# A macaron layer of two feed-forward passes and an S4D mixer: no side work behind the last two tiles of an ordinary block's second wide layer, and steps one fourteenth larger

## The chip, the core and the metric

The kernel runs on one core of a Trainium2 chip. The time is that of the device for one execution, in microseconds (us). A core has five engines that matter here, each with its own queue of instructions, taken in order: TensorE (PE in the profile; its weight loads are PEld), VectorE (DVE), ScalarE (ACT), GpSimd (POOL), and SyncE (SP), which only issues DMAs here. They run side by side and wait for one another through semaphores.

## The reference

The input x is (4, 1024, 256): four sequences of 1,024 tokens with 256 channels. Three residual steps follow one another:

```
x = x + 0.5 * ffn(layernorm(x))
x = x + mix(layernorm(x))
x = x + 0.5 * ffn(layernorm(x))

ffn(x):   h = silu(x @ w1.T * s1) * (x @ w2.T * s2)    # 256 -> 1024
          h = gelu(h @ h1.T * s_h1)                    # 1024 -> 1024
          h = gelu(h @ h2.T * s_h2)                    # 1024 -> 1024
          return h @ w3.T * s3                         # 1024 -> 256
mix(x):   K[d, l] = 2 Re sum_n C'[d, n] exp(dtA[d, n] * l)
          y = irfft(rfft(x, 2L) * rfft(K, 2L))[:L]     # along the tokens, L = 1024
          return gelu(y) @ W.T + b
```

Both passes have the same weights. All matrices of the ffn are ternary (-1, 0, 1). Everything is float32, and the gelu is the exact one.

## The kernel before

**Blocks.** Each ffn pass is cut into eight blocks of 512 tokens: f0 to f7 in the first pass, g0 to g7 in the second. They are worked one after another: f0 to f7, g0, g1 as ordinary blocks (`ffn`), then (g2, g3), (g4, g5), (g6, g7) as pairs (`ffn_pair`), which save matmuls by a product of Strassen's kind. Activations are held with features on the 128 partitions and the 512 tokens along the free axis. A wide layer (1,024 features) is thus eight tiles of 128 x 512, m = 0 to 7.

**A wide tile.** Each activation is kept as two tiles for TensorE's fp32r format: a high part, which is a cast of the value, and a low part, which is the value less the high part. Since the weights are ternary, a matmul with each part gives the product to about the accuracy of float32. `linear` (L363) issues for a tile of layer 2 or 3 16 matmuls (eight blocks of input features, two parts each) into one bank of PSUM, L366. ScalarE then takes the gelu (L399), ScalarE casts it to the high part (L401), VectorE subtracts for the low part (`low_part`, L309). In layer 1 there are two banks, `pa` and `pb`, of eight matmuls in all; silu is L384, the product with `pb` L385, the cast L389. Tiles are named by layer and block: p2_f0_3, g2_f0_3, h2_f0_3 are the bank, the gelu and the two parts of tile 3 of layer 2 in f0. The profile leaves the numbers out: p_f, g_f, h_f, and ha_f for layer 1.

**The end of a block.** `last_squares` (L604 to L632) multiplies the eight tiles of layer 3 by w3: two banks `po`, 16 matmuls each, L617. ScalarE scales them (L628), VectorE transposes (L629), POOL adds the residual (L630), and stores follow. The next block's layer 1 comes right after `po` on TensorE; its operand xt is cut into parts by `parted` (casts L356, low parts L309), once the last tile of the block before is done.

**Side work.** All else is done beside the wide tiles of ordinary blocks. After each tile of layers 2 and 3 two things are called:

- `ahead()` moves the preparation of the next block on by one step: load of x, mean and variance on VectorE (L155), the root for them on ScalarE (`rstd`, L289), scaling (L155), transposes into squares of 32 (`sq`) and a way through DRAM (L339).
- `tick()` (L1237) hands out a portion of the rest. The rest is a generator, `aside`: `kernel_steps`, the table of powers for the S4D kernel (during f0 to f2); its spectrum; and for each of the four sequences `mix`, as soon as its two f blocks are done. `fillers` (checks that the weights are what the kernel takes them for) fill up where `aside` has nothing.

The part of `kernel_steps` that runs in f0's layer 3 is `powers`: for a group of channels an angle `a` and a factor `e` on VectorE, an exp on ScalarE (L820), the reduction of the angle in four VectorE operations with `k` as helper, a sine and a cosine on ScalarE (L740, L741), the products with `e` and with `c_dt`, and from them the tiles `qd`. The names are e_0_0, a_0_0, k_0_0 for the fine powers and e_b_0, a_b_0, k_b_0, then e_b_32, a_b_32, k_b_32, qd_32, qd_48 for the coarse ones. Gelu, sine, exp and root each have a table of their own in ScalarE; where one follows another, an ACT_TABLE_LOAD stands between them.

How much a tick hands out is a matter of counting: every VectorE operation of side work adds OP_WORK (130) and its columns to `work_done` (L144 to L153), and a tick runs the generator

```
allowed = min(allowed, work_done) + (STEP_WORK_2 if f7 is done else STEP_WORK)
while work_done < allowed:   next(aside) ...
```

The order of the instructions on each engine is then set by the scheduler of the language, which takes the program in this order and may put an instruction ahead of others on its engine when it reckons that it is ready earlier; pools of 19 `half` tiles and 15 `ring` tiles bound how far ahead.

At the end of the program a flag tells whether a weight was not ternary; then everything is run again in a plainer way. With these inputs it is not.

Of the kernel before, what the change touches and what calls it, by code (L numbers as in the profile page):

```python
# [23 lines left out]
KH = HID // P  # L24
# [10 lines left out]

STEP_WORK, STEP_WORK_2, OP_WORK, MIN_WORK = 3600, 3400, 130, 300
PAUSE = "pause"
N_CHECKS = 44  # L40

# [67 lines left out]
def macaron_layers(  # L109
# [54 lines left out]
    def bank(name):  # L164
        return psum.tile([P, 512], F32, tag="ps", name=name)

    def half(name, *shape, dtype=F32):

        return work.tile([P, *(shape or (512,))], dtype, tag="half", name=name, bufs=19)

    def ring(name, *shape, dtype=F32):

        return work.tile([P, *shape], dtype, tag="ring", name=name, bufs=15)
# [133 lines left out]
    def low_part(t, src):  # L307

        return nc.vector.tensor_tensor(t[:, 1, :], src, t[:, 0, :].bitcast(F32), ALU.subtract)  # L309
# [52 lines left out]
    def linear(ps, w, m, acts):  # L362
        n = len(acts)  # L363
        for k in range(n):
            for part in range(parts):
                nc.tensor.matmul(  # L366
                    ps,
                    w[:, k, m * P : (m + 1) * P],
                    acts[k][:, part, :],
                    start=(k == 0 and part == 0),  # L370
                    stop=(k == n - 1 and part == parts - 1),
                )

    def ffn(xt, src, dst, blk, name, tick, ahead, final):


        ha = []
        for m in range(KH):
            pa, pb = bank(f"pa_{name}_{m}"), bank(f"pb_{name}_{m}")
            linear(pa, w1_sb, m, xt)  # L380
            linear(pb, w2_sb, m, xt)
            g = half(f"g_{name}_{m}")
            t = ring(f"ha_{name}_{m}", parts, TB, dtype=wide)
            nc.scalar.activation(g, pa, AF.Silu, scale=sc_sb[:, 0, m : m + 1])  # L384
            nc.vector.scalar_tensor_tensor(  # L385
                g if split else t[:, 0, :], pb, sc_sb[:, 1, m : m + 1], g, ALU.mult, ALU.mult
            )
            if split:
                nc.scalar.copy(t[:, 0, :], g)  # L389
                low_part(t, g)  # L390
            ha.append(t)
        for layer, w in ((2, h1_sb), (3, h2_sb)):
            hb = []
            for m in range(KH):
                ps = bank(f"p{layer}_{name}_{m}")
                linear(ps, w, m, ha)
                t = ring(f"h{layer}_{name}_{m}", parts, TB, dtype=wide)
                g = half(f"g{layer}_{name}_{m}") if split else t[:, 0, :]
                nc.scalar.activation(g, ps, AF.Gelu, scale=sc_sb[:, layer, m : m + 1])  # L399
                if split:  # L400
                    nc.scalar.copy(t[:, 0, :], g)  # L401
                    low_part(t, g)
                hb.append(t)
                ahead()
                if layer == 2 or m < KH - 1:
                    tick()
            ha = hb
        ahead(last=True)
        if name == "f0":
            nc.scalar.mul(w3s_half, w3s_half, 0.5)  # L410
        if final:
            last_tokens(ha, src, dst, blk, name)
        else:
            last_squares(ha, src, dst, blk, name)()
# [188 lines left out]
    def last_squares(acts, src, dst, blk, name, first=0):  # L603


        rest = []
        for k in range(DC):
            xr = half(f"xr_{name}_{k}", TB // SQ, SQ)
            for c in range(P // SQ):
                nc.sync.dma_start(xr[c * SQ : (c + 1) * SQ], in_squares(src, blk, k, c))  # L610
            rest.append(xr)
        banks = [bank(f"po_{name}_{k}") for k in range(DC)]
        order = [(first + k) % KH for k in range(KH)]
        for o, ps in enumerate(banks):
            for k in order:
                for part in range(parts):
                    nc.tensor.matmul(  # L617
                        ps,
                        w3_sb[:, k, o * P : (o + 1) * P],
                        acts[k][:, part, :],  # L620
                        start=(k == order[0] and part == 0),
                        stop=(k == order[-1] and part == parts - 1),
                    )

        def end():
            for k, ps in enumerate(banks):
                o, y = half(f"o_{name}_{k}"), half(f"y_{name}_{k}", TB // SQ, SQ)
                nc.scalar.activation(o, ps, AF.Identity, scale=w3s_half[:, k : k + 1])  # L628
                nc.vector.transpose(y, o.rearrange("p (n s) -> p n s", s=SQ))  # L629
                nc.gpsimd.tensor_tensor(y, rest[k], y, ALU.add)  # L630
                for c in range(P // SQ):
                    stores.dma_start(in_squares(dst, blk, k, c), y[c * SQ : (c + 1) * SQ])  # L632

        return end

    def last_tokens(acts, src, dst, blk, name):

        rest = {}
        for i in (0, 2):
            rest[i] = half(f"xr_{name}_{i}", 2, D)  # L640
            nc.sync.dma_start(rest[i], tokens(src, blk, i, 2))

        def result(ps, i, n):

            for e in range(n):
                for k in range(KH):
                    for part in range(parts):
                        nc.tensor.matmul(  # L648
                            ps[:, e * D : (e + 1) * D],
                            acts[k][:, part, (i + e) * P : (i + e + 1) * P],  # L650
                            w3_sb[:, k, :],
                            start=(k == 0 and part == 0),
                            stop=(k == KH - 1 and part == parts - 1),
                        )

        def finish(ps, y, xr, i, n, add_on):
            nc.vector.scalar_tensor_tensor(
                y,
                ps.rearrange("p (e d) -> p e d", e=n),
                0.5,  # L660
                w3s_sb[:, None, :].to_broadcast([P, n, D]),
                ALU.mult,
                ALU.mult,
            )
            add_on.tensor_tensor(y, xr, y, ALU.add)
            nc.sync.dma_start(tokens(dst, blk, i, n), y)

        y = half(f"y_{name}_0", 2, D)
        ps = bank(f"po_{name}_0")
        result(ps, 0, 2)  # L670
        finish(ps, y, rest[0], 0, 2, nc.gpsimd)
        y = half(f"y_{name}_2", 2, D)
        for e in range(2):
            ps = bank(f"po_{name}_{2 + e}")
            result(ps, 2 + e, 1)
            finish(ps[:, 0:D], y[:, e : e + 1, :], rest[2][:, e : e + 1, :], 2 + e, 1, nc.vector)
# [568 lines left out]
    def tick():  # L1245


        nonlocal ticks, allowed, work_done
        ticks += 1
        allowed = min(allowed, work_done) + (  # L1250
            STEP_WORK_2 if ("f", n_blocks - 1) in done else STEP_WORK
        )
        while work_done < allowed:
            at = work_done
            if next(aside, PAUSE) is PAUSE:
                for _ in range(2):
                    if len(done) > 8 and allowed - work_done > OP_WORK + TB:
                        next(fillers, None)
                break
            if work_done == at:  # L1260
                work_done += MIN_WORK
# [10 lines left out]
    for n, unit in enumerate(units):  # L1272
# [6 lines left out]
        def ahead(last=False):  # L1279
            if last:  # L1280
                done.extend(("last layer", *b[::-1]) for b in upcoming)
            for step in steps:
                next(step, None)
# [15 lines left out]
        with tc.issue_after(last_split.ins) if n == 0 else nullcontext():  # L1299
            if pair:  # L1300
                blks = [b for _, b in unit]
                ffn_pair(operands, src, dst, blks, names, tick, ahead, final)
            else:
                ffn(operands[0], src, dst, blk, names[0], tick, ahead, final)
# [81 lines left out]
```

## Time and profile before

| | |
|---|---|
| median of the runs | 1368.81 us (1368.12 to 1369.08, 3 runs) |
| the profiled execution | 1368.22 us, its span 1366.4 us |
| mean granted TensorE clock | 0.999 of full speed |
| L366 (wide layers of ordinary blocks), each matmul 128x128 by 128x512 | 391 ns mean |
| L617 `po_f` matmuls | 256, 60.7 us busy |
| ACT_TABLE_LOAD before L399, L289, L384, L820, L740 | 35, 19, 10, 8, 8 of them, 1283 ns each |

The span is the time between the first and the last instruction that the profile shows; the execution's own time has some two microseconds around it. Busy times of TensorE are modelled: matmuls are pipelined, one lasts 391 ns from its start to its modelled end, but the next starts 227 ns after it. Lines of groups give the line of the source, the engine, the operation, output<-input, sizes and number, and after the bar busy time, mean duration, and the idle time before them with what ended it. Lines of waits give engine, tile and line, what was waited for, then microseconds in total, times, and the longest.

### The profile page before, as it was taken

The page shows a single profiled execution, that of the slowest core. Times are in us where ns is not written, and L with a number is a line of the kernel's source. Part 1 is how long each engine was busy: PE and PEld are TensorE (multiplying, and loading weights), DVE is VectorE, ACT ScalarE, POOL GpSimd, SP SyncE. Part 2 cuts the span into 40 slices and gives each one's busy share as a digit, 9 for nine tenths or more (in the row PEclk, how much of TensorE's full clock was granted, in tenths as well). Part 3 has the DMA queues.
Part 4 walks back from the last instruction along what each step waited for, and adds up shares of the span by engine and source line. Part 5 has one row for each costly group of instructions (what it writes and reads, how often), then busy time and mean ns, then how long its engine had stood idle before and what let it go on. Part 6 is the DMA issues. An engine that isn't in the chain of part 4 may idle for free.

```text
span 1366.4 us, 18201 instructions
## 1 busy us (share of the span) xinstructions
PE 1351.8 (99%) x6300; PEld 1125.2 (82%) x6300; DVE 1008.8 (74%) x1886; ACT 776.4 (57%) x1236; POOL 297.1 (22%) x454
## 2 busy tenths in 40 slices
PE   9999999999999999999999999999999999999997
PEld 7888878888888888887888887888888888888886
DVE  6997885749865887668855799658885778568654
ACT  5985966454444543534545745436776476656663
POOL 4440220421205213420214012052300430040002
PEclk9999999999999999999999999999999999999999
DMA  9440121414125236454054342352655145521441
GB/s 354 114 141 3 31 62 39 146 33 124 39 93 204 59 108 188 125 183 120 20 169 115 115 154 47 115 166 83 208 165 168 31 139 181 170 66 62 160 148 34
DMA packets 121670, 160.00 MB, mean 117 GB/s; under 512 B 73872, under 2 KB 84112, under 8 KB 116192
## 3 DMA queue, kind: packets, MB, share of 16 engines
q1 hardware_dynamic: 99296, 99.41, 23.8%
q0 software_dynamic: 22000, 59.07, 13.9%
q8 instruction: 51, 0.84, 0.3%
q14 instruction: 51, 0.42, 0.1%
q10 hardware_dynamic: 272, 0.26, 0.1%
HBM read 120.95 MB, written 37.75 MB: 116 GB/s over the span
## 4 chain that ended last, share of the span: by engine, by line
PE 50%; DVE 4%; issue 1%; DMA 0%; ACT 0%; SPq 0%; DVEq 0%; POOLq 0%; POOL 0%; ACTq 0%
PE p_g L366 7%; PE p3a_g L510 6%; PE p2a_g L510 6%; PE p2x_g L510 5%; PE p3x_g L510 5%; PE p_f L366 4%; PE pa_g L366 4%; PE pb_g L366 4%; PE po_g L617 3%; PE pi L1134 1%; PE pw L1159 1%; DVE y L155 1%; PE po_f L617 1%; PE po_g L648 1%; PE pa_f L366 1%; PE pb_f L366 1%
## 5 line engine op out<-in xcount | busy, mean ns | idle before, releaser
L366 PE MATMUL p_f<-ha_f,h_sb 128*128 128x512 f32 x1024 | 238.7, 392 | 0.1
L366 PE MATMUL p_f<-h_f,h_sb 128*128 128x512 f32 x1024 | 237.1, 391 | 0.0
L366 PEld LDWEIGHTS p_f<-h_f,h_sb 128*128 128x128 f32 x1024 | 192.1, 188 | 39.7
L366 PEld LDWEIGHTS p_f<-ha_f,h_sb 128*128 128x128 f32 x1024 | 191.4, 188 | 40.4 <-DVE ha_f L309 0.8
L399 ACT ACTIVATE g_f<-p_f,sc_sb 128x512 f32<-128x512 f32 x128 | 87.4, 689 | 210.2 <-PE p_f L366 178.6
L309 DVE TENSOR_TENSOR h_f<-g_f,h_f 128x512 fp32r<-128x512 f32 x128 | 88.1, 691 | 113.4 <-ACT h_f L401 113.2
L630 POOL TENSOR_TENSOR y_g<-xr_g,y_g 128x512 f32<-128x512 f32 x14 | 19.9, 1431 | 323.8 <-DVE y_g L629 310.1
L401 ACT CAST h_f<-g_f 128x512 fp32r<-128x512 f32 x128 | 78.4, 619 | 3.1
L524 ACT ACTIVATE h_g<-h_g,sc_sb 128x512 f32<-128x512 f32 x72 | 52.0, 724 | 43.9 <-DVE h_g L480 43.6
L339 POOL DMA_DIRECT2D moved<-sq_f x56 | 30.6, 554 | 197.8 <-DVE sq_f L155 197.8
L366 PE MATMUL pa_f<-xt_f,w_sb 128*128 128x512 f32 x256 | 70.5, 391 | 1.8 <-DVE xt_f L356 1.2
L339 POOL DMA_DIRECT2D moved<-sq_g x64 | 34.9, 552 | 167.5 <-DVE sq_g L155 166.3
L366 PE MATMUL pb_f<-xt_f,w_sb 128*128 128x512 f32 x256 | 70.0, 389 | 0.0
L366 PE MATMUL pa_g<-xt_g,w_sb 128*128 128x512 f32 x256 | 68.9, 389 | 0.0
L366 PE MATMUL pb_g<-xt_g,w_sb 128*128 128x512 f32 x256 | 68.9, 389 | 0.0
L617 PE MATMUL po_f<-h_f,w_sb 128*128 128x512 f32 x256 | 60.7, 391 | 1.6 <-ACT h_f L401 0.9
L385 DVE SCALAR_TENSOR_TENSOR g_f<-pb_f,sc_sb,g_f 128x512 f32<-128x512 f32 x64 | 46.6, 746 | 19.7 <-ACT g_f L384 10.0
L366 PE MATMUL p_g<-ha_g,h_sb 128*128 128x512 f32 x256 | 59.4, 391 | 0.1
L366 PE MATMUL p_g<-h_g,h_sb 128*128 128x512 f32 x256 | 59.3, 391 | 0.0
L366 PEld LDWEIGHTS pa_f<-xt_f,w_sb 128*128 128x128 f32 x256 | 48.0, 188 | 12.8 <-DVE xt_f L356 1.6
L617 PEld LDWEIGHTS po_f<-h_f,w_sb 128*128 128x128 f32 x256 | 47.6, 188 | 13.0 <-DVE h_f L309 2.0
L399 ACT ACTIVATE g_g<-p_g,sc_sb 128x512 f32<-128x512 f32 x32 | 22.1, 690 | 60.8 <-PE p_g L366 50.3
(302 smaller groups left out, 2887.9 us busy)
## 6 DMA issues: line engine op xcount, KB each, us to landing
w<-q SPq DMA_DIRECT2D x42, 1024.0 KB, 5.0
q<-s POOLq DMA_DIRECT2D x40, 256.0 KB, 4.4
h_sb<-in_h_dram POOLq DMA_DIRECT2D x8, 1024.0 KB, 14.4
given<-in_h_dram SPq DMA_DIRECT2D x32, 256.0 KB, 3.4
kr<-k_hat SPq DMA_DIRECT2D x20, 256.0 KB, 2.8
ki<-k_hat SPq DMA_DIRECT2D x20, 256.0 KB, 3.1
q<-h_sb POOLq DMA_DIRECT2D x16, 256.0 KB, 4.8
xr_f<-in_x_dram SPq DMA_DIRECT2D x64, 64.0 KB, 2.5
```

What stands on the lines that cost most here:

```text
L155: return op(dst, *args, **kwargs)
L309: return nc.vector.tensor_tensor(t[:, 1, :], src, t[:, 0, :].bitcast(F32), ALU.subtract)
L339: stores.dma_start(moved[k].rearrange("(c r) a q -> a r c q", r=SQ)[a], sq[a * SQ : (a + 1) * SQ].rearrange("r c j s -> r c (j s)"),)
L366: nc.tensor.matmul(ps, w[:, k, m * P : (m + 1) * P], acts[k][:, part, :], start=(k == 0 and part == 0), stop=(k == n - 1 and part == parts ...
L385: nc.vector.scalar_tensor_tensor(g if split else t[:, 0, :], pb, sc_sb[:, 1, m : m + 1], g, ALU.mult, ALU.mult)
L399: nc.scalar.activation(g, ps, AF.Gelu, scale=sc_sb[:, layer, m : m + 1])
L401: nc.scalar.copy(t[:, 0, :], g)
L510: nc.tensor.matmul(ps, weights[:, c, m * P : (m + 1) * P], ops[c][:, part, :], start=(first and c == 0 and part == 0), stop=(c == QK - 1 a ...
L524: nc.scalar.activation(o, src, AF.Gelu, scale=sc_sb[:, layer, m : m + 1])
L617: nc.tensor.matmul(ps, w3_sb[:, k, o * P : (o + 1) * P], acts[k][:, part, :], start=(k == order[0] and part == 0), stop=(k == order[-1] an ...
L630: nc.gpsimd.tensor_tensor(y, rest[k], y, ALU.add)
L648: nc.tensor.matmul(ps[:, e * D : (e + 1) * D], acts[k][:, part, (i + e) * P : (i + e + 1) * P], w3_sb[:, k, :], start=(k == 0 and part == ...
```

## The change

In an ordinary block, a tick followed each of the 16 wide tiles of layers 2 and 3 but the last: 15 ticks. Now none follows the last two: 14 ticks. The portion of a tick grows by about a fourteenth, from 3,600 to 3,850 units, and after f7 from 3,400 to 3,640. `ahead()` is called after every tile as before. The pair blocks have ticks of their own, with the larger portion too.

```diff
-STEP_WORK, STEP_WORK_2, OP_WORK, MIN_WORK = 3600, 3400, 130, 300
+STEP_WORK, STEP_WORK_2, OP_WORK, MIN_WORK = 3850, 3640, 130, 300
...
                     low_part(t, g)
                 hb.append(t)
                 ahead()
-                if layer == 2 or m < KH - 1:
+                if layer == 2 or m < KH - 2:
                     tick()
             ha = hb
         ahead(last=True)
```

## The prediction

> **What bounds the kernel now.** I read the page first, then the waits of TensorE, then the queues of the engines around the ends of the ordinary blocks. From the page:
>
> ```profile
> span 1366.4 us, 18201 instructions
> ...
> PE 1351.8 (99%) x6300; PEld 1125.2 (82%) x6300; DVE 1008.8 (74%) x1886; ACT 776.4 (57%) x1236; POOL 297.1 (22%) x454
> ...
> PE   9999999999999999999999999999999999999997
> ...
> ACT  5985966454444543534545745436776476656663
> ...
> L399 ACT ACTIVATE g_f<-p_f,sc_sb 128x512 f32<-128x512 f32 x128 | 87.4, 689 | 210.2 <-PE p_f L366 178.6
> L309 DVE TENSOR_TENSOR h_f<-g_f,h_f 128x512 fp32r<-128x512 f32 x128 | 88.1, 691 | 113.4 <-ACT h_f L401 113.2
> ```
>
> TensorE is full in every slice, and neither the number nor the size of its matmuls changes. So only the time in which it stands still can change. ScalarE and VectorE have room on the average, but the third ACT digit (68 to 102 us, the end of block f0 in it) is an 8 after a 9: there ScalarE is nearly full. The waits of TensorE that belong to ends of blocks:
>
> ```profile
> PE pa_f L366 <- DVE xt_f L356: 1.2, 1, 1.2
> PE po_f L617 <- ACT h_f L401: 0.9, 1, 0.9
> PE po_f L617 <- DVE h_f L309: 0.7, 1, 0.7
> PE po_g L617 <- DVE h_g L309: 0.6, 1, 0.6
> PE po_g L617 <- ACT h_g L401: 0.3, 1, 0.3
> ```
>
> They are small. Matmuls start 0.2267 us apart (64 of them fill 14.52 us in the chain), so the 32 of `po` need 7.25 us. Laid against the starts in the timeline, which also shows what the pipelined ends hide, the ends of blocks stand still for 0.35 (f0), 2.15 (f1), 0.06 (f4), 1.42 (f6) and 1.47 us (g0), and the starts of layer 2 in f1 and g1 for 0.48 and 0.36. That is 5.45 us at block ends: all that the change can win by its own idea, 6.3 with the two starts. One such end, f1, in TensorE's timeline (start, length):
>
> ```profile
> 171.46 6.51 PE L617 MATMUL po_f<-h_f,w_sb 128*128 128x512 f32 x28
> 178.86 0.73 PE L617 MATMUL po_f<-h_f,w_sb 128*128 128x512 f32 x2 [0.89 <-ACT h_f L401]
> 180.31 0.72 PE L617 MATMUL po_f<-h_f,w_sb 128*128 128x512 f32 x2 [0.72 <-DVE h_f L309]
> ```
>
> 28 matmuls run, the last four wait for the last tile of layer 3: its cast, then its low part.
>
> **What a last tile needs.** Gelu 0.69, cast 0.62 and low part 0.69 us end 2.26 us after the tile's last matmul if nothing else stands in the queues. 14 matmuls of the next stage can run before it is needed (3.17 us). So side work put between these three costs nothing up to 0.9 us, and more when earlier matmuls can be put ahead.
>
> **The change, part by part.** A tick lets side work run until 3,850 units instead of 3,600 are counted (3,640 instead of 3,400 after f7). Over a block it is 14 x 3,850 = 53,900 against 15 x 3,600 = 54,000: as much work, 250 units more per tile. A 512-column VectorE operation counts 642 and starts 0.60 us after its predecessor, so a tile gets about 0.25 us more, and the tile m=6 of layer 3 gives up about 3.4. No matmul and no VectorE, POOL or SP operation is added or removed. What is added are ScalarE's table loads, 92 to 96 in the built program: f4 +3, f6 and g0 +2 each, g1 +1, less two each in f2 and g2; f0 keeps 22, in another order. A load takes 1.28 us (below), so 5 us more on an engine with 590 us idle; it costs only where a wide tile waits behind it. On TensorE some 130 of 5,892 instructions change places, among them the 16-matmul groups of the mix (3.45 us each, f5's last into f6's layer 2, g1's from layer 3 into layer 2); they take the same time there. On SP and POOL the same DMAs are issued, some in another order: the last quarter of x_f3 ahead of stores of squares, the kr, ki, given and xr loads up to a tile earlier or past one another. These land 2.5 to 3.4 us after their issue and are read a tile (3.63 us) or more later; I cost them at nothing, and at one such landing, 3.4 us, if a late one ever stood ahead of a low part.
>
> The scheduler decides the order on each engine, so I walked the queues of the built program with durations of this trace: gelu 0.69 (0.59 behind another), cast 0.62, table load 1.28, sine pair 1.25, exp 0.63, root 0.30; VectorE 0.69 (0.60), `qd` 0.43, x_f3's scaling 0.33.
>
> *Blocks f1, f6, g0 (the gain).* In f1 the sine group of tile 5 is issued one tile earlier, so the low parts of tiles 6 and 7 come at 177.85 and 178.45 instead of 178.9 and 180.25; they are needed at 176.9 and later, which leaves 0.6 of the 2.15: **-1.5**. In f6 the two stand at 641.3 and 641.9, needed at 642.5 and 643.6, and the cast of `xt_f7` is ahead of them now: **-1.4**. In g0, 826.0 and 826.6, needed from 825.1: some 0.55 left of 1.47: **-0.9** (-1.5 to +0.5, since ScalarE gets two loads more there). f4: **-0.06**. No other block end stood still, and none does in the walk.
>
> *Block f0 (the loss).* Here it is ScalarE's order that counts. Its timeline at the end of f0 before:
>
> ```profile
> 82.78 1.28 ACT L289 ACT_TABLE_LOAD   x1
> 84.08 0.30 ACT L289 ACTIVATE rstd_f<-mv_f,eps 128x4 f32<-128x4 f32 x1
> 84.28 0.61 ACT L401 CAST h_f<-g_f 128x512 fp32r<-128x512 f32 x1
> 84.91 1.28 ACT L740 ACT_TABLE_LOAD   x1
> 86.20 0.63 ACT L740 ACTIVATE a_b<-a_b 128x512 f32<-128x512 f32 x1
> 86.74 0.71 ACT L741 ACTIVATE k_b<-k_b,cst_sb 128x512 f32<-128x512 f32 x1
> ```
>
> The cast at 84.28 is h3_f0_7's; the sine pair of a_b_32, k_b_32 and the root of f3 come behind it, at no cost. In the built program both stand ahead of g3_f0_6, because the larger step of tile 5 reaches them. Between the first gelu of layer 3 and that last cast there are 11 table loads instead of 8 (+3.9 us), three sine pairs instead of two (+1.25) and two roots instead of one (+0.3): +5.45. And the stretch starts later. The exp e_0_0 with its two loads moves ahead of g2_f0_7, so h2_f0_7 is ready near 62.95 instead of 58.58; TensorE's order allows for that with 46 matmuls ahead of its first use (63.3) instead of 27. So TensorE does not wait, but p3_f0_0 closes only then, and ScalarE's layer 3 starts at 64.4 instead of 60.3 (+4.1). Its idle bits of before (0.74) are filled. The last cast ends at 84.9 + 4.1 + 5.45 - 0.74 = 93.7, that of tile 6 at 93.2. On VectorE the sine pair's products, the rest of x_f3 and four `qd` (4.4 us, from 90.4) stand ahead of the low parts of tiles 6 and 7: ready at 95.5 and 96.1. TensorE finishes p3_f0_7 at 81.9 and the 24 matmuls of tiles 0 to 5 near 88.5, since tile 5's own low part comes at 87.5; stands still to 93.3, again to 95.5, and leaves `po` near 97.1 instead of 89.48: **+7.7**. Both ends: +5.5 if VectorE gets round to the low parts as soon as the casts are there (tail 93.7 + 0.69 + 0.6), +9.3 if h2_f0_7 is 1.5 us later than walked. The walk's own bookkeeping stands nearer the middle, which I take. Then f0's side work no longer reaches into f1, whose start loses its 0.48: **-0.45**.
>
> *The clock.* No gap of TensorE exceeds 1.4 us before, so the trace shows what a long one does only at its end:
>
> ```profile
> core 0: us, PE busy (x) PEld busy (x) DVE busy (x) ACT busy (x) POOL busy (x), PEclk, DMA share, GB/s
> ...
> 1355.00:1360.00 5.00, 3.86 (x33) 3.65 (x31) 2.39 (x5) 0.00 (x0) 3.86 (x5) 1.00 0.33 87
> 1360.00:1366.00 6.00, 0.00 (x0) 0.00 (x0) 0.00 (x0) 0.00 (x0) 0.00 (x0) 0.76 0.27 73
> ```
>
> The last matmul ends at 1358.9; a mean of 0.76 over six us is full clock to about 1363.1 and half after: 4.3 us of idleness. The gap foreseen at f0 is 4.8. The Trainium skill ("TensorE: Matmul & The Clock Gate", What's actually happening) puts the drop to half at an idle window of about 3.4 us and the return after a busy one as long. By the page the gap trips for certain, and a 3.4 us window at half speed loses 1.7. By the row it trips just barely or not: 0. At most two windows, 3.4. I take **+1.0**.
>
> *The loads.* The Trainium skill ("ScalarE: Activation LUTs", What ACT_TABLE_LOAD costs) gives 1.28 us and a drain of 1.38 for every switch, which speaks against this change: three switches more in f0 would be 8.0 us instead of 3.9, the sum +8.5. In the timeline above the next operation follows 0.02 us behind the load (84.08, 86.20), so there is no drain here, and I take 1.28.
>
> **The sum.** +7.7 - 0.45 - 1.5 - 0.06 - 1.4 - 0.9 = +3.4, with the clock +4.4. On the profiled execution, 1368.22 (span 1366.4 and 1.8 around it), 1372.6; that execution lies 0.6 under the median of the runs, 1368.81, which the prediction goes by: **1373.2 us**. The pair blocks keep TensorE's order, and by then no side work is left for a tick.
>
> **Rivals.** *A: the change does what it says everywhere*, f0 too: the tiles before last find empty queues and 4.6 to 5.4 us of waits go: about 1364, faster. For it: f1, f6 and g0 in the waits. Against it: the ScalarE order in f0. It decides if f0's `po` ends by 93 instead of 97.1; below that the gains outweigh it.
>
> *B: f0 loses less*, +5.5, because VectorE is not behind, and the clock holds: +1.2, about 1370, not to be told from no change (0.2%, 2.7 us, is about what a measurement of this kernel can tell). For it: VectorE has 26% idle over the span. Against it: it is busy throughout 52.9 to 82 in f0.
>
> *C: larger steps are late elsewhere too.* Before the last tile of layer 2 the walk leaves 0.2 us in f5 and g0 and 0.5 for tile 6 in f7: a load more ahead of one costs about 1 us each, and the clock its two windows: +3.4 + 2 + 2.4 to 3.4, about 1377. Against it: these waits are filled in TensorE's order by the next tile's first 14 to 18 matmuls.
>
> **How the numbers follow.** Likeliest (1371.5 to 1375.5) 0.52; B 0.22; C 0.16; A 0.08; the rest, 0.02, further up. Range: half of B and nearly all of C stay in it, 1368.4 to 1377.6. Faster: A, 0.08. Within 0.2% (1366.1 to 1371.5): B, 0.22. Slower: 0.70.
>
> **What would show it.** In the profile after: a wait of `po_f` for h_f of about 4.8 us and a second of about 2.2, both in f0 (88 to 97 us); `po_g` and `pa_f <- xt_f L356` waits gone or under 0.6; f1's `po` below 0.7; a granted clock under 1.00 in a window of 90 to 102 us if the clock term is real. Wrong would be: no wait over 3 us near 90 (then A or B), a full clock through 90 to 102 (then about 1372), or new waits at starts of layer 3 (C).

## The result and the profile after

| | before | after |
|---|---|---|
| median of the runs | 1368.9 us (1368.12 to 1370.22, 8 runs) | 1373.51 us (1373.05 to 1374.58, 8 runs) |
| ratio to before | | 1.0033, 95% interval 1.0024 to 1.0041 |
| the profiled execution, its span | 1368.22, 1366.4 us | 1374.58, 1372.8 us |
| granted clock, mean of the span | 0.999 | 0.994 |

The changed kernel is 4.6 us slower by the medians; its profiled execution is the slowest of the eight, so the two spans lie 6.4 us apart. Its page, the lines that answer to those of before:

```profile
span 1372.8 us, 18195 instructions
...
PE 1354.4 (99%) x6300; PEld 1126.8 (82%) x6300; DVE 1007.2 (73%) x1886; ACT 780.4 (57%) x1240; POOL 297.5 (22%) x454
...
PE   8989999999999999999999999999999999999997
...
ACT  5785875454363543544544746345776566656663
PEclk9989999999999999999999999999999999999999
```

TensorE's third slice (69 to 103 us) is an 8, and so is the clock's. ScalarE has four instructions more, the table loads. The waits of TensorE:

```profile
PE po_f L617 <- ACT h_f L401: 4.6, 1, 4.6
...
PE po_f L617 <- DVE h_f L309: 2.3, 3, 1.0
...
PE po_g L617 <- DVE h_g L309: 0.3, 1, 0.3
```

One wait of 4.6 us is new. The small ones have shrunk: `po_g` is down to 0.3, `pa_f <- xt_f L356` of 1.2 is gone. TensorE's timeline puts the new wait at the end of f0:

```profile
82.11 4.54 PE L617 MATMUL po_f<-h_f,w_sb 128*128 128x512 f32 x18
87.24 1.66 PE L617 MATMUL po_f<-h_f,w_sb 128*128 128x512 f32 x6 [0.58 <-DVE h_f L309]
93.46 1.22 PE L617 MATMUL po_f<-h_f,w_sb 128*128 128x512 f32 x2 [4.57 <-ACT h_f L401]
95.63 2.93 PE L617 MATMUL po_f<-h_f,w_sb 128*128 128x512 f32 x6 [0.95 <-DVE h_f L309]
98.36 1.91 PE L366 MATMUL pa_f<-xt_f,w_sb 128*128 128x512 f32 x4
```

Layer 1 of f1 starts at 98.36; before it started at 89.48. The last two lines show a second thing: six matmuls of `po` take 2.93 us, and the next four matmuls begin 0.427 us apart, not 0.227. The granted clock says why. In the windows below the columns are the length, the busy time of TensorE, its weight loads, VectorE, ScalarE and POOL (with their instructions in brackets), then the clock, and last what the DMAs did:

```profile
84.00:88.00 4.00, 3.40 (x14) 2.19 (x13) 4.00 (x9) 3.95 (x7) 0.00 (x0) 1.00 0.00 0
88.00:92.00 4.00, 0.89 (x4) 0.40 (x3) 3.96 (x10) 3.96 (x5) 0.00 (x0) 0.88 0.72 114
92.00:96.00 4.00, 1.59 (x3) 0.87 (x4) 3.93 (x9) 1.92 (x4) 0.00 (x0) 0.50 0.11 17
96.00:100.00 4.00, 4.00 (x10) 3.10 (x10) 3.43 (x7) 2.08 (x3) 1.16 (x1) 0.50 0.00 0
100.00:104.00 4.00, 4.00 (x16) 3.21 (x15) 1.11 (x3) 1.97 (x3) 3.69 (x6) 0.84 0.32 66
```

The clock is halved from 91.0 to 101.3 us. From 84 to 92 VectorE and ScalarE are full, and TensorE waits for them. ScalarE's timeline up to the cast that ends the long wait:

```profile
86.17 1.28 ACT L289 ACT_TABLE_LOAD   x1
87.47 0.30 ACT L289 ACTIVATE rstd_f<-mv_f,eps 128x4 f32<-128x4 f32 x1
87.78 1.28 ACT L740 ACT_TABLE_LOAD   x1
89.08 0.63 ACT L740 ACTIVATE a_b<-a_b 128x512 f32<-128x512 f32 x1
89.61 0.71 ACT L741 ACTIVATE k_b<-k_b,cst_sb 128x512 f32<-128x512 f32 x1
90.34 1.28 ACT L399 ACT_TABLE_LOAD   x1
91.63 1.26 ACT L399 ACTIVATE g_f<-p_f,sc_sb 128x512 f32<-128x512 f32 x2
92.79 1.13 ACT L401 CAST h_f<-g_f 128x512 fp32r<-128x512 f32 x2
```

Root and sine pair with three table loads stand ahead of the gelus of tiles 6 and 7, whose matmuls had ended at 78.7 and 82.3.

### The profile page after: what moved, and what is told of

Read it like the earlier page. It is cut to its first block, busy times and chain, and to the rows that moved or that the text cites. A ratio compares the mean times of both kernels' runs of the same rounds, so it can differ in the third digit from the quotient of the medians.

```text
span 1372.8 us, 18195 instructions
## 1 busy us (share of the span) xinstructions
PE 1354.4 (99%) x6300; PEld 1126.8 (82%) x6300; DVE 1007.2 (73%) x1886; ACT 780.4 (57%) x1240; POOL 297.5 (22%) x454
## 4 chain that ended last, share of the span: by engine, by line
PE 86%; DVE 5%; issue 1%; ACT 1%; POOL 0%; DVEq 0%; POOLq 0%; ACTq 0%
PE p_f L366 27%; PE p2a_g L510 6%; PE p3a_g L510 6%; PE p_g L366 6%; PE p3x_g L510 5%; PE p2x_g L510 5%; PE pa_g L366 4%; PE pb_g L366 4%; PE pa_f L366 4%; PE pb_f L366 4%; PE po_f L617 4%; PE po_g L617 3%; PE pi L1134 2%; PE pf_m L956 2%; PE pw L1159 2%; PE pk L883 1%
```

## The experiments

All were timed beside runs of the kernel before on the same chip (median 1369.15 to 1369.49), so ratios compare best. The theory: f0 alone loses, because larger steps put the exp and the sine pair a tile earlier; the ends of f1, f6 and g0 gain; a halved clock adds to the loss. The rivals are that the loss is spread over the blocks, that leaving out the tick is to blame, that one engine alone sets f0's end, and that the clock costs nothing.

| kernel | median, us | ratio, 95% interval |
|---|---|---|
| the change (measured again) | 1373.34 | 1.0030 (1.0019 to 1.0042) |
| everywhere but in f0 | 1364.97 | 0.9965 (0.9952 to 0.9979) |
| in f0 alone | 1377.86 | 1.0056 (1.0042 to 1.0070) |
| larger steps alone | 1397.10 | 1.0195 (1.0181 to 1.0209) |
| change, in f0 only the tick left out | 1371.37 | 1.0016 (1.0009 to 1.0024) |
| change, f0 without sine and exp tables | 1368.51 | 0.9997 (0.9989 to 1.0006) |
| change, six VectorE operations fewer in f0 | 1371.95 | 1.0023 (1.0014 to 1.0033) |
| the same, one table load fewer | 1370.48 | 1.0009 (1.0002 to 1.0016) |
| change and 18 matmuls more in f0 | 1372.87 | 1.0025 (1.0016 to 1.0034) |
| change and 26 matmuls more in f0 | 1371.51 | 1.0017 (1.0010 to 1.0025) |

### Where: f0 or everywhere

The change everywhere but in f0:

```diff
-                if layer == 2 or m < KH - 2:
+                if layer == 2 or m < KH - (1 if name == "f0" else 2):
...
-            STEP_WORK_2 if ("f", n_blocks - 1) in done else STEP_WORK
+            STEP_WORK_2 if ("f", n_blocks - 1) in done
+            else STEP_WORK if ("f", 0) in done else STEP_WORK_F0     # 3600
```

> The change everywhere but in f0, which keeps 15 steps of 3,600. Theory (the whole loss sits at the end of f0): f0 looks as before (wait at its end 0.3 us), the waits at the ends of f1, f6 and g0 and at the start of g1 go as they went in the changed kernel (about 1.1, 1.4, 0.9 and 0.4 us), so 1365.1 us, range 1364.3 to 1366.3, and the granted clock stays full until the last matmul. Rival (larger steps are late in many places, f0 is only one): 1368 to 1373 us with waits outside f0.

And in f0 alone (the same edit the other way round: 3,850 and KH - 2 in f0; 3,600, 3,400 and KH - 1 after it):

> The change in f0 alone (14 steps of 3,850 there), all later blocks as before. Theory: f0's loss without the later gains, 1373.5 + 3.8 = 1377.3 us, range 1376 to 1378.5, with a wait of 4 to 5 us at the end of f0 and half clock for 7 to 10 us after it. Rival (the loss is spread over the blocks): below 1373.5.

Measured were 1364.97 and 1377.86. The order of VectorE's and ScalarE's instructions in f0 is that of before in the one and that of the change in the other. Waits of TensorE without f0's part:

```profile
PE po_f L617 <- DVE h_f L309: 0.7, 1, 0.7
...
PE po_g L617 <- DVE h_g L309: 0.3, 1, 0.3
```

and with f0's part alone:

```profile
PE po_f L617 <- ACT h_f L401: 5.5, 2, 4.6
...
PE po_f L617 <- DVE h_f L309: 2.2, 3, 1.0
...
PE pa_f L366 <- DVE xt_f L356: 0.6, 1, 0.6
PE po_g L617 <- DVE h_g L309: 0.6, 1, 0.6
PE po_g L617 <- ACT h_g L401: 0.3, 1, 0.3
```

The wait of 4.6 us goes when f0 is left as it was, and the small waits of before come back when the later blocks are. The loss is 0.56% in f0 and the gain 0.35% elsewhere; their difference, 0.21%, is near the change's own 0.30% within the intervals. The version without f0's part is faster than both kernels. One expectation failed in its profiled execution: there the clock was halved once, from 9.5 to 12.9 us, at the beginning of the program. That execution took 1366.63 us, 1.7 more than the median, which is what 3.4 us at half speed lose.

### Which edit: the larger step or the omitted tick

Larger steps alone (3,850 and 3,640, ticks as before), as a diff to the change:

```diff
-                if layer == 2 or m < KH - 2:
+                if layer == 2 or m < KH - 1:
```

> The larger steps alone; a tick still follows the last tile but one. Theory (the larger step brings the sine pair of a_b_32 and the exp e_0_0 one tick earlier in f0, and that is the loss; the omitted tick is the gain at f1, f6 and g0): f0 loses as in the changed kernel, the waits at f1, f6 and g0 stay, 1376 to 1379 us. Rival (the omitted tick makes f0's loss by crowding the others): f0's end as before, about 1369 us.

The f0 part came true: there TensorE waits 4.15 us and then 1.65 and 1.86, and ScalarE has the same order of tables. The sum did not, by 20 us: a tick behind the last tile but one is far worse with the larger steps than with the old ones. TensorE's waits:

```profile
PE pa_f L366 <- DVE xt_f L356: 6.0, 2, 3.8
PE po_f L617 <- DVE h_f L309: 4.3, 4, 1.9
PE po_f L617 <- ACT h_f L401: 4.1, 1, 4.1
PE pa_g L366 <- DVE xt_g L356: 3.9, 1, 3.9
...
PE pk L883 <- DVE p L155: 2.0, 1, 2.0
```

At the ends of f4, f6 and g0 it waits 2.2, 3.8 and 3.9 us for the next block's operand, whose casts stand on VectorE behind the side work. Each long wait takes a halved clock with it: 31 us of half clock besides that at the end of the run. With 15 x 3,850 = 57,750 units a block holds 7% more side work than before. So the omitted tick is what makes the larger step bearable.

The omitted tick alone, tried in f0 (later blocks as in the change):

```diff
-STEP_WORK, STEP_WORK_2, OP_WORK, MIN_WORK = 3850, 3640, 130, 300
+STEP_WORK_F0, STEP_WORK, STEP_WORK_2, OP_WORK, MIN_WORK = 3600, 3850, 3640, 130, 300
...
-            STEP_WORK_2 if ("f", n_blocks - 1) in done else STEP_WORK
+            STEP_WORK_2 if ("f", n_blocks - 1) in done
+            else STEP_WORK if ("f", 0) in done else STEP_WORK_F0
```

> The changed kernel with steps of 3,600 in f0, so there only the tick behind the last tile but one is left out (later blocks as changed). Theory (the larger step makes f0's loss, the omitted tick hardly any): ScalarE keeps the order of before up to the cast of tile 6; only the sine pair of a_b_32 comes ahead of the last cast, which costs TensorE about 1 us at the end of f0; no half clock: 1365 to 1366.5 us. Rival (leaving out the tick crowds the tiles before): 1370 us or more, with a wait over 3 us in f0.

The part on f0 came true, the time did not: it is the rival's, for another reason. At the end of f0 TensorE waits 0.40 us for a low part, 0.55 and 0.20 more by the start of f1's layer 1, and the clock stays full: the 4.6 us are gone, so the omitted tick is not what crowds f0. But the run is at 1371.37, since the 3,600 units that f0 no longer does are late much later, in g1, where TensorE waits for a low part:

```profile
916.75 2.43 PE L617 MATMUL po_g<-h_g,w_sb 128*128 128x512 f32 x10
923.04 2.52 PE L617 MATMUL po_g<-h_g,w_sb 128*128 128x512 f32 x6 [3.87 <-DVE h_g L309]
```

VectorE's timeline says what holds it:

```profile
921.24 0.43 DVE L356 CAST xt_g<-xf_g 128x512 fp32r<-128x512 f32 x1 [5.20 <-DMA xf_g<-moved]
921.96 0.43 DVE L356 CAST xt_g<-xf_g 128x512 fp32r<-128x512 f32 x1 [0.29 <-DMA xf_g<-moved]
922.30 0.68 DVE L309 TENSOR_TENSOR h_g<-g_g,h_g 128x512 fp32r<-128x512 f32 x1
```

The mix ends later, so the first pair's operand comes later out of DRAM; its cast stands at the head of VectorE's queue for 5.2 us, and the low part that TensorE waits for stands behind it. Leaving out the tick in all blocks with the old steps wasn't tried: the last mix is then not through when the pairs begin, which the program does not allow.

### What fills f0's end: ScalarE or VectorE

Six VectorE operations fewer ahead of tile 6's low part, ScalarE's order unchanged:

```diff
-                for t, m in ((c, 0), (i, 1)):
+                for t, m in ((c, 0), (i, 1)) if d0 != 32 else ():
                     by = c_dt[:, m, d0 : d0 + some, None] ...
...
-                        tt(t[part, :, h, :], c[part, ch], i[part, ch], ALU.add)
+                        if d0 != 32: tt(...)     # counted as work either way
```

> The changed kernel without six VectorE operations ahead of h3_f0_6's low part: the products with c_dt and the sums into qd_32 and qd_48 are left out (that part of the output is not the reference's), 2.9 us, all else in the same order. Theory (ScalarE comes right behind VectorE): the low part of tile 6 then waits for its cast, which ends at 93.4, and is done at 94.1 instead of 95.6, tile 7 at 94.7 instead of 96.2; the first wait at 88.9 stays, the second shrinks from 1.35 to under 0.4; 1.5 us less than the changed kernel, more if a window of half clock goes with it: 1370.3 to 1372. Rival (VectorE alone sets the end): 2.9 us less in f0.

And one table load fewer besides:

```diff
-        sin_cos(c, a)
+        sin_cos(c, a, AF.Identity if name == "b_32" else AF.Sin)
```

> The kernel with the six VectorE operations left out, and the sine pair of a_b_32 computed as an identity too, so that one table load of 1.28 us fewer stands ahead of g3_f0_6; all else in the same order (those parts of the output are not the reference's). Theory: the casts of tiles 6 and 7 come 1.3 us earlier, and TensorE with them: the first wait shrinks from 4.6 to 3.3 us, 1.3 us less than without the six operations alone. Rival (ScalarE isn't on the path): no change against the run with the six operations left out.

TensorE's timelines, first with the six operations fewer, then with the load fewer too:

```profile
93.51 3.54 PE L617 MATMUL po_f<-h_f,w_sb 128*128 128x512 f32 x8 [4.55 <-ACT h_f L401]
96.88 1.07 PE L366 MATMUL pa_f<-xt_f,w_sb 128*128 128x512 f32 x4
```

```profile
92.03 3.78 PE L617 MATMUL po_f<-h_f,w_sb 128*128 128x512 f32 x8 [3.15 <-ACT h_f L401]
95.64 1.07 PE L366 MATMUL pa_f<-xt_f,w_sb 128*128 128x512 f32 x4
```

Tile 6's low part ends at 94.18, tile 7's at 94.78, as expected (95.58 and 96.18 in the change): of 2.9 us taken from VectorE 1.4 come through. The second wait is gone, as expected, and in both of these runs the half clock lasts 3.4 us instead of 10.2. The rest needs ScalarE: with its load gone the long wait is 1.4 us shorter and layer 1 of f1 starts 1.24 us earlier. So both engines set f0's end, VectorE last by 1.4 us, ScalarE right behind it.

Without any sine or exp table in f0's layer 3:

```diff
-        nc.scalar.activation(e, e, AF.Exp)
+        plain = name in ("0_0", "b_0", "b_32")
+        nc.scalar.activation(e, e, AF.Identity if plain else AF.Exp)
...
-        sin_cos(c, a)
+        sin_cos(c, a, AF.Identity if plain else AF.Sin)
```

> The changed kernel, but the sines and exps of the three groups of powers in f0's layer 3 are computed as identities, so that they need no table (that part of the output is not the reference's): 88 loads instead of 96, seven of the eight fewer in f0's layer 3, and the order on the engines shifts where the scheduler reckons with them. Theory (ScalarE's loads are what fills f0's end): the wait at the end of f0 goes to under 1 us, no half clock, about 1364.5 us. Rival (VectorE's queue alone sets it): the wait stays above 4 us, 1371 us or more.

Neither theory nor rival came true, the result lies between the two: one wait of 2.35 us for a low part (VectorE) is left, and 3.4 us of half clock behind it. The order moves with this edit, VectorE's too, so it shows how much hangs on the loads together with what they move (4.8 us by the medians), not the loads by themselves.

### What the clock costs

Unused matmuls in f0, ahead of `po`, where TensorE has time for them:

```diff
         ahead(last=True)
+        if name == "f0":
+            fill = bank("fill")
+            for i in range(N_FILL):          # 18, then 26; the result is not used
+                nc.tensor.matmul(fill, h2_sb[:, 0, 0:P], ha[0][:, 0, :], ...)
```

> The changed kernel with 18 matmuls more (4.1 us of TensorE, their result unused) between p3_f0_7 and po of f0, where TensorE would otherwise stand still for 4.7 us a little later. The end of f0 is set by the low parts of tiles 6 and 7 on VectorE either way, so they cost nothing. Theory (the long gap halves the clock, and the slow matmuls cost 1.6 to 3.0 us): full clock from 84 to 104 us, 1370.5 to 1372.0 us although there is more work. Rival (the half clock is hidden in waits): 1373.5 us. Rival (the gap isn't what halves the clock): the clock drops all the same.

> The changed kernel with 26 matmuls more (5.9 us) ahead of po in f0, so that TensorE comes to h3_f0_6 just when its cast ends and only the wait for VectorE (1.4 us) is left in its window. Theory (what halves the clock is a window of 3.4 us in which TensorE is idle for about half of it or more): full clock from 80 to 110 us, layer 1 of f1 begins near 97.1 instead of 98.4, and the run is 1.3 to 2.7 us below the changed kernel measured beside it. Rival (18 matmuls showed that the clock falls in any case): half clock for 3.4 us, less than 1 us below.

With 18 the gap is cut into waits of 1.68 and 1.42 us. The clock stays full past the first and drops after the second, once. With 26 only the second is left, 1.20 us, and the clock stays full. Windows with 18 matmuls:

```profile
92.60:96.00 3.40, 1.10 (x4) 0.62 (x5) 3.33 (x8) 1.34 (x3) 0.00 (x0) 1.00 0.03 5
96.00:99.40 3.40, 3.40 (x10) 2.62 (x9) 3.15 (x7) 1.78 (x3) 0.44 (x1) 0.50 0.00 0
```

and with 26:

```profile
93.89:97.31 3.42, 2.23 (x10) 1.51 (x9) 3.36 (x8) 0.49 (x2) 0.00 (x0) 1.00 0.00 0
97.31:100.72 3.41, 3.41 (x16) 2.77 (x16) 2.50 (x5) 3.38 (x5) 1.68 (x2) 1.00 0.00 0
```

So 18 matmuls were a miss on the full clock, and moved the time by too little to tell (1.0025 against 1.0030 to 1.0033). With 26 the forecast holds. Beside them the change was measured again:

> The changed kernel once more, beside the one with 26 matmuls. Theory: a ratio of 1.003 to before as at first; half clock after the end of f0 for one to three windows of 3.4 us, by where the window falls.

It came out at 1373.34 against 1371.51, again with half clock for 10.2 us: 5.9 us more work on TensorE makes the run 1.8 us shorter. VectorE sets the end of f0 at the same time in both (the last six matmuls of `po` start at 95.61 with 26 more and at 95.63 in the change), so this is the price of the half clock. With 26, layer 1 of f1 starts at 97.12.

## Why the prediction was right

Forecast was 1373.2, measured 1373.51. Term by term, from the starts of matmuls in the traces of before and after, but for the two rows that name another source:

| step | forecast | measured |
|---|---|---|
| end of f0, at full clock | +7.7 | +7.4 (from the end of layer 3's matmuls to layer 1 of f1 15.04 us, in the run with 26 matmuls more, against 7.60 before) |
| start of f1's layer 2 | -0.45 | -0.48 |
| end of f1 | -1.5 | -1.1 (2.15 to 1.02) |
| end of f4, f6, g0 | -0.06, -1.4, -0.9 | -0.06, -1.4, -0.9 |
| start of g1's layer 2 | none | -0.36 |
| clock | +1.0 | +1.8 (medians, the change against 26 matmuls more) |
| sum | +4.4 | +4.9 |

The medians of all runs lie 4.6 us apart. The mechanism was right in each term that was foreseen but the clock's. That the sum comes so near is in part luck: the terms miss by -0.3, +0.4, -0.36 and +0.8, and these cancel.

*f0.* The walk foresaw the casts of tiles 6 and 7 at 93.2 and 93.7 and their low parts at 95.5 and 96.1; in the trace the low parts end at 95.58 and 96.18, and the two casts at about 93.4 and 93.9. Layer 3 of ScalarE starts at 64.63 (64.4). The waits of 4.6 and 0.95 us are the "about 4.8 and about 2.2" of the prediction, the second shorter since two slow matmuls fill part of it. One reason was put wrongly: the prediction has the sine pair reached by the step of tile 5. By the program's count of work it is the step of tile 4 that issues it now, and the step of tile 5 did before; the exp e_0_0 likewise goes from tile 7 of layer 2 to tile 6. The order that was walked was the built one, so the number did not suffer.

*f1*: the gain was taken 0.4 too high: the low parts of tiles 6 and 7 end 6.97 and 7.57 us after the start of layer 3's last matmul, where the walk had 6.62 and 7.22. The wait that is left there is 0.74 us, just above the 0.7 that the prediction gave as a sign. The gain at the start of g1's layer 2 was not foreseen.

*The clock* is the term that was mis-sized, within its bounds (0 to 3.4). The forecast weighed the length of a gap against a threshold and allowed two windows at most. What counts is how much TensorE did in a window that lies fixed in time (see the end), and in both profiled executions of the change it was three windows, 10.2 us. Part of these falls into the waits. In the profiled execution the half clock cost 2.6 us (`po` of f1 starts at 181.14, with 26 matmuls more in f0 at 178.56), more than by the medians.

*The loads.* In the rows shown above the next operation follows 0.01 to 0.02 us behind each load, so the drain of 1.38 us that the Trainium skill ("ScalarE: Activation LUTs", What ACT_TABLE_LOAD costs) adds to a switch is absent in the changed kernel too. One load taken from ScalarE's queue moved TensorE's long wait by 1.4 us, where 2.66 would have been the page's.

*Rival A*, gains everywhere, is what the version without f0's part does: 1364.97, where A's own figure was 1364. *Rival C*, stalls elsewhere, did not come in the change, but did with larger steps alone.

## What to carry to other kernels

When work is handed out in portions beside a full engine, the average of work per tile says little; look for the one stage in which the helpers are already full, and walk their queues there in the built order, table loads included. Here it is layer 3 of f0, where before the change VectorE was busy for 20.40 and ScalarE for 19.55 of 20.50 us:

```profile
64.40:84.90 20.50, 20.50 (x91) 16.81 (x90) 20.40 (x46) 19.55 (x26) 10.85 (x21) 1.00 0.69 245
```

A change that helps the other stages may be worth making with that stage left out: 4.5 us gained by medians instead of 4.6 lost. And count the work that a stage no longer does: it comes due somewhere else, here in g1, 800 us later.

## What the runs showed of the hardware

The clock of TensorE does not need a long idle gap to be halved. The Trainium skill ("TensorE: Matmul & The Clock Gate", What's actually happening) speaks of an idle window of about 3.4 us. The length agrees: half clock lasted 3.4 us in the runs with one window and 10.2 in the change. But the window was not idle: 1.10 us busy of 3.40 sufficed with 18 matmuls, and even 1.80 of 3.40 in the run with the change in f0 alone (end of f1):

```profile
187.10:190.50 3.40, 1.80 (x7) 0.90 (x6) 3.33 (x9) 1.60 (x3) 0.00 (x0) 1.00 0.33 53
190.50:194.00 3.50, 3.50 (x10) 2.68 (x10) 2.78 (x6) 2.60 (x3) 1.23 (x1) 0.51 0.63 99
```

The kernel before has the same two waits there (0.89 and 0.72 us in the timeline of the prediction) with a full clock in its profile. Where the window falls decides. In every trace with several changes of the clock they lie whole multiples of 3.413 us apart (in the change 91.01, 101.25 and 1367.60 us, that is 3 and 371 of them), so the windows form a fixed grid, which can be counted back from any change. In the run with the change in f0 alone both waits fall into one window of that grid. In the kernel before, the grid (counted back from the drop at its end, 1363.07 us) parts them, with 11 matmuls begun in the one window and 10 in the other:

```profile
175.23:178.64 3.41, 2.73 (x13) 1.92 (x11) 3.40 (x7) 2.42 (x3) 0.00 (x0) 1.00 0.00 0
178.64:182.06 3.42, 2.48 (x10) 1.76 (x11) 3.36 (x9) 1.31 (x3) 0.00 (x0) 1.00 0.68 106
```

Counted on this grid, the twelve traces agree without exception after the first 10 us of the program. Count the matmuls that begin in a window, each by its columns (512 for one of 128x512). All 26 windows at full clock with at most 2,560 columns, five such matmuls, were followed by half clock. All the others had at least 3,072, six matmuls, and were followed by the full one. With 18 matmuls more it was four in the window up to 96.0 us, with the change in f0 alone five, with 26 matmuls more eight. This was counted in the traces that were there; no run varied it by itself.

Two waits of under a microsecond can thus cost up to 1.7 us more in slow matmuls (an estimate: half of a window). Whether they do hangs on where the grid lies, which differs from execution to execution (in the change the clock dropped at 91.01 us, measured again at 91.30).
